# A four-layer graph network in fp32: where layer 0's bias per node is formed and added

## The chip, the cores and the metric

The kernel runs on one core of a Trainium2 chip. The metric is device time in microseconds for one launch, the median of three runs: 1666.78 us (1666.35 to 1666.91). Everything is computed in fp32.

## The reference

Eight batches of 2048 nodes with 64 features pass through four graph layers, each with a residual connection and a layer norm. `adj` is a dense 2048x2048 matrix. Only layer 0 bears on the change:

```python
def _L0_gnn_ref(x, A, embedding, weight, bias):   # K=3, D=16, 64 -> 64 features
    w = jnp.einsum('nd,dkio->nkio', embedding, weight)
    b = jnp.einsum('nd,do->no', embedding, bias)
    As = [eye(N), A, 2.0 * (A @ A) - eye(N)]
    x_g = jnp.einsum('knm,bmc->bnkc', jnp.stack(As, 0), x)
    out = jnp.einsum('bnki,nkio->bno', x_g, w)
    return out + b
...
x = _layernorm(x + _L0_gnn_ref(x, adj, ...), axis=-1)
...
x = _layernorm(x + _L1_gnn_ref(...))   # two products with adj, ReLU after each
x = _layernorm(x + _L2_gnn_ref(...))   # one product with adj, own and neighbour weights
x = _layernorm(x + _L3_gnn_ref(...))   # two products with adj
```

Each node has its own weights and its own bias, both mixed from 16 shared ones by the node's embedding. The bias of a node, `b[n]`, is a vector of 64 numbers, the same for all eight batches; it is a sum of 16 terms.

## The kernel before

**Data.** `xy` holds two copies of the node features in SBUF, slot 0 and slot 1, as 16 node tiles of 128 nodes (partitions) by 512 columns (8 batches of 64). The 8 batches are worked in 4 pairs of 128 columns. Layer 0 keeps x in slot 0, where the layer's output is gathered, and `A x` in slot 1.

**Products.** A product with `adj` uses a two-level scheme of Strassen's kind: on each level seven multiplications of sums of blocks in place of eight. The sums of adj's blocks are formed once by VectorE during the first product (`prepare`, L634) and written to DRAM (`comb`, by GpSimd's DMA queue, L649), from which all later products read them. A later product (`product`, L216) consists of seven inner products A11, S1, A12, S2, S4, S3, A22 in this order; each is seven multiplications on TensorE (L277, 3.43 us each), whose partial sums VectorE adds up from PSUM (L228) in two banks, and forms sums of x for the ones to come.

**Layer 0's first product** runs in four slices of adj (`plain_slice` for slice 0, `fast_slice` for slices 1 to 3). Its result comes out transposed and is turned back by TensorE (`to_nodes`, L465) through the pool `p_tn` of two PSUM banks, which `two_level` (L818) also uses for its partial products. Scheduling is by a planner, except where `keep_in_program_order` pins an instruction to its place on its engine.

**The bias before.** The embedding, transposed, and the 16 shared biases are loaded by ScalarE's DMA queue (L728, L733). In slice 1 TensorE forms all 16 node tiles' biases by 16 matmuls (`biases`, L737) into two banks, the pool `p_b`. In slice 3 VectorE adds them to x in four instructions of 128x2048 (`join_bias`, L766), one per quarter of x; then `centered` (L1028) takes the mean over each node's 64 features away from x, which a layer norm would do later, also on VectorE.

**Layer 0's second product and the node weights.** The second product, of slot 1, begins at the end of the slices. When an inner product has finished a quarter of the result, its four blocks are handed to `feature0` (L1090). For each of the block's four node tiles TensorE multiplies the three terms of x with the 16 shared weights, in two halves of 8, into a PSUM tile `y` (L1109; the pool `p_y` has three). VectorE scales the first half's 8 products by the node's embedding and adds them onto slot 0 (L1119). ScalarE scales the second half's 8 products into an SBUF tile `s` (L1123; two buffers), which GpSimd adds up and joins to slot 0 (L1128, L1130). The features are not mixed with the multiplications: they run in stretches after S2 (four blocks, node tiles 0 to 7, batches 0 to 3), after S3 (four, the same tiles, batches 4 to 7) and after A22 (eight blocks, tiles 8 to 15). A layer norm of two blocks follows some steps after its second block; in layer 0 GpSimd squares (L503) and VectorE does the rest.

`center` (L586) is a reduction and a subtraction on VectorE that takes the mean over the last axis away from a tile of weights; `sum_wn` (L1068) uses it for the 16 shared weights.

Of the kernel before, what the change touches and what calls it, by code (L numbers as in the profile page):

```python
# [9 lines left out]
F32 = mybir.dt.float32  # L10
AF = mybir.ActivationFunctionType
ALU = mybir.AluOpType
# [4 lines left out]
P = 128  # L17
# [87 lines left out]
def kernel(  # L105
# [4 lines left out]
    slices: bass.AP,  # L110
    blocks: bass.AP,
    emb: bass.AP,
    embT: bass.AP,
    w_l0: bass.AP,
    b_l0: bass.AP,
    w_l1: bass.AP,
# [8 lines left out]
    N = x.shape[0] * x.shape[1]  # L125
    BF = x.shape[2]
    D = emb.shape[2]
    F = b_l0.shape[1]
    B = BF // F
    NT = N // P  # L130
    NG = N // GW
# [453 lines left out]
    if True:  # L585
# [126 lines left out]
            yield  # L712

        with tc.tile_pool(name="p_n", bufs=4, space=PSUM) as p_n, tc.tile_pool(
            name="p_tn", bufs=2, space=PSUM
        ) as p_tn, tc.tile_pool(name="p_b", bufs=1, space=PSUM) as p_b, tc.tile_pool(
            name="xs", bufs=1
        ) as xs:

# [2 lines left out]
            rise = p_tn.tile([P, TG, P], F32, tag="pt", name="rise")  # L722
            for k in range(11):
                nc.tensor.matmul(rise[:, k % TG, :], zero, zero, start=True, stop=True)

            bias0 = small.tile([P, F], F32, tag="bias0", name="bias0")
            for k in range(2):
                nc.scalar.dma_start(bias0[k * F : k * F + D], b_l0)  # L728
            pb = p_b.tile([P, NT, F], F32, tag="pb", name="pb")
            e_tile = small.tile([P, TG, 4, F], F32, tag="sq", name="eT").rearrange("p t b f -> p (t b f)")  # L730
            eT = [e_tile[g // 2 * F : g // 2 * F + D, ts(g % 2, GW)] for g in range(NG)]
            for g in range(NG):
                nc.scalar.dma_start(eT[g], embT[:, ts(g, GW)])  # L733

            def biases():

                for t in (h * NT // 2 + k for k in range(NT // 2) for h in range(2)):  # L737
                    g = t // TG
                    tc.keep_in_program_order(nc.tensor.matmul(
                        pb[:, t, :], eT[g][:, ts(t % TG, P)], bias0[g // 2 * F : g // 2 * F + D],  # L740
                        start=True, stop=True,
                    ))
                yield

            def xq(h, c):

                v = xy[:, 0, h * NT // 2 : (h + 1) * NT // 2, c * 4 * F : (c + 1) * 4 * F]
                return v.rearrange("p (t h) c -> p t h c", h=2)
# [9 lines left out]
            def sums_of_x(n):  # L758
# [3 lines left out]
                    (T[2], xq(1, 1), xq(0, 1)), (T[3], xq(1, 0), T[1]),  # L762
                )[n]
                pin(nc.vector.tensor_tensor(out, a, b, ALU.subtract))

            def join_bias(h, c):  # L766
                v = xq(h, c).rearrange("p t h (b f) -> p (t h) b f", f=F)
                bias = pb[:, h * NT // 2 : (h + 1) * NT // 2, :].unsqueeze(2)
                bias = bias.to_broadcast([P, NT // 2, B // 2, F])
                tc.keep_in_program_order(nc.vector.tensor_tensor(v, v, bias, ALU.add))  # L770

            def load_chunks(ns, *js):
                if ns < TG:
# [122 lines left out]
            def fast_slice(ns, ch, held, rest):  # L896


                outers = {}
                parts = prepare(ns, ch, outers)  # L900

                def raw(I, J):
                    return lambda j, m: ch[2 * J + j][:, m, 2 * I : 2 * I + 2]

                def summed(q):
                    return lambda j, m: outers[q][:, :, j, ts(m, P)]

                def x_of(h, c):
                    return lambda k, p: xcol(0, h * NT // 2 + k, 2 * c + p)

                def t_of(n):
                    return lambda k, p: T[n - 1][:, k // 2, k % 2, ts(p, 2 * F)]

                def mul(ps, a, b, start=True, steps=2):

                    for p in range(2):
                        for k in range(NT // 2):
                            nc.tensor.matmul(  # L918
                                ps[:, ts(p, GW // 2)], b(k, p), a(k // TG, k % TG),
                                start=(start and p == k == 0), stop=(k == NT // 2 - 1),  # L920
                                skip_group_check=True,
                            )
                        if p < steps:
                            pump.step()
                    return ps

                hT = {}

                def done(blk, ps, plus):
                    ih, c = blk // 2, blk % 2  # L930
                    for p in range(2):
                        if 2 * c + p not in hT:
                            hT[2 * c + p] = new_h()
                        nc.vector.tensor_tensor(
                            hT[2 * c + p][:, ts(ih, GW // 2)], ps[:, ts(p, GW // 2)],
                            plus[:, ts(p, GW // 2)], ALU.add,
                        )

                def plus(tag, a, b):
                    u = sums.tile([P, GW], F32, tag=tag, name=tag)  # L940
                    nc.vector.tensor_tensor(u, a, b, ALU.add)
                    return u

                next(parts)
                for _ in rest:
                    pass
                next(parts)

                p2 = mul(bank(), raw(0, 1), x_of(1, 0), steps=1)
                q3 = new_out("u3")  # L950
                two_level(
                    lambda i, j: lambda m: ch[2 + j][:, m, 2 + i], outers[A22], b4, t4, by_blocks(q3)
                )
                load_chunks(ns + 1, 2, 3)
                for job in held:
                    pump.add(back(*job))
                next(parts)
                pa = mul(bank(), raw(0, 0), x_of(0, 0))
                p1 = sums.tile([P, GW], F32, tag="p1", name="p1")
                nc.scalar.copy(p1, pa)  # L960
                nc.vector.tensor_tensor(q3, q3, p1, ALU.add)
                done(0, p2, p1)
                if ns == TG - 1:
                    join_bias(0, 1)
                next(parts)
                pc = mul(bank(), summed(S1), t_of(1))
                next(parts)
                load_chunks(ns + 1, 0, 1)
                if ns == 1:
                    sum_weights(w3)  # L970
                elif ns == TG - 1:
                    join_bias(0, 0)
                pb_ = mul(bank(), summed(S2), t_of(2))
                u2 = plus("u2", pb_, p1)
                nc.vector.tensor_tensor(u2, pc, u2, ALU.add)
                nc.vector.tensor_tensor(p1, pc, p1, ALU.add)
                next(parts)
                pe = mul(bank(), summed(S4), x_of(1, 1))
                done(1, pe, u2)
                if ns == TG - 1:  # L980
                    join_bias(1, 0)
                mul(pb_, summed(S3), t_of(3), start=False)

                done(2, pb_, q3)
                done(3, pb_, p1)
                return [hT[p] for p in range(NP)]

            last_pairs = []
            for ns in range(TG):
                ch = [chunks.pop((ns, j)) for j in range(NG)]  # L990
                if ns == 0:
                    outers = {}
                    parts = prepare(ns, ch, outers)
                    for _ in range(2):
                        next(parts)
                    first4 = plain_slice(ns, ch, outers)
                    next(first4)
                    sums_of_x(0)
                    sums_of_x(1)
                    next(parts)  # L1000
                    next(first4)
                    sums_of_x(2)
                    sums_of_x(3)
                    sums_t(b4, t4)
                    next(first4)
                    next(parts)
                    hT = next(first4)
                    next(parts)
                    w3 = load_weights()
                    load_chunks(1, *AHEAD)  # L1010
                    pump.add(biases())
                else:
                    hT = fast_slice(ns, ch, held, parts if ns == 1 else ())
                for p in range(NP):
# [3 lines left out]
                for p in range(NP):  # L1018
# [3 lines left out]
                        last_pairs.append(hT[p])  # L1022
                    else:
                        pump.add(back(ns, p, hT[p]))
            join_bias(1, 1)
            pump.drain()

        def centered(h, c):  # L1028
# [13 lines left out]
        if True:  # L1042
# [11 lines left out]
                yield  # L1054

            pump.add(last_back())
            for h, c in ((0, 0), (0, 1), (1, 1), (1, 0)):
                pump.add(centered(h, c))
            e_sb = l0y.tile([P, NT, D], F32, tag="e_sb", name="e_sb")
            nc.gpsimd.dma_start(e_sb, emb)  # L1060

            wn = l0y.tile([P, 3, D, F], F32, tag="wn", name="wn")
            pieces += [
# [26 lines left out]
            def feature0(g, p, hT):  # L1090
# [7 lines left out]
                for k in range(TG):  # L1098
# [1 line left out]
                    acc = xy[:, 0, t, ts(p, 2 * F)].rearrange("p (b f) -> p b f", f=F)  # L1100


                    s = l0y.tile([P, DH, 2, F], F32, tag="s", name="s", bufs=2)
                    for h in range(2):
                        y = p_y.tile([P, 2, DH * F], F32, tag="y", name="y")
                        for n in range(3):
# [22 lines left out]
                        n //= 2  # L1129
                    nc.gpsimd.tensor_tensor(acc, acc, s[:, 0], ALU.add)  # L1130
                    yield


            RUNS = {A12: 1, S2: NP, S3: NP}
# [131 lines left out]
```

## Time and profile before

| | |
|---|---|
| median of three runs | 1666.78 us |
| the profiled execution | 1666.76 us |
| its span in the profile | 1665.0 us |
| busy in the span: PE, PEld, DVE, ACT, POOL | 1656.7, 1060.6, 965.9, 276.0, 246.1 us |
| TensorE's granted clock | 0.999 |
| slices (layer 0's first product) | 0 to 211 us |
| A11 to S2 of layer 0's second product | 211 to 309 us |
| features, four blocks | 309 to 392 us |
| S4 and S3 | 392 to 440 us |
| features, four blocks | 440 to 522 us |
| A22 and the next product's A11 | 522 to 570 us |
| features, eight blocks | 570 to 736 us |
| layers 1 to 3 | 736 to 1665 us |

The engines are PE (TensorE's matmuls), PEld (its weight loads), DVE (VectorE), ACT (ScalarE), POOL (GpSimd) and SP (a queue that here only starts DMAs). A line of the time line gives start, duration, engine, source line, operation, what it writes and reads, the shape and the count of merged instructions, and in brackets how long the engine was idle before and what it waited for. A matmul in fp32 stands in the trace as two records. In lines that group instructions, the numbers behind the bar are busy us and the mean ns of one, then the idle time before them and what ended it. In lines of a stretch stand its bounds, its length, each engine's busy time with its count, TensorE's granted clock, the DMA engines' busy share and GB/s. L12 is line 12 of the kernel.

### The profile page before, as it was taken

How to read it: one execution, taken by the hardware profiler on the slowest of the kernel's cores; microseconds unless marked ns; L12 is line 12 of the kernel's file. 1: busy time of each engine (PE TensorE's matmuls, PEld its weight loads, DVE VectorE, ACT ScalarE, POOL GpSimd, SP SyncE). 2: the span in 40 equal slices, each digit the busy share in tenths (PEclk: the TensorE clock that was granted, in tenths of full speed). 3: DMA queues.
4: the chain of work that ended last, by engine and by line, in shares of the span. 5: the costliest groups of instructions: out<-in, count | busy, mean ns of one | idle time of the engine just before them, and what ended most of it. 6: DMA issues, size and time to landing. Idle time of an engine off the chain costs nothing.

```text
span 1665.0 us, 21271 instructions
## 1 busy us (share of the span) xinstructions
PE 1656.7 (100%) x8414; PEld 1060.6 (64%) x8414; DVE 965.9 (58%) x1737; ACT 276.0 (17%) x810; POOL 246.1 (15%) x332
## 2 busy tenths in 40 slices
PE   9999999999999999999999999999999999999998
PEld 5988844444444444444454455599998455579998
DVE  5986895656456456655434365873668344453657
ACT  0200110242142144430010011220001011100001
POOL 1221200254155056550000000000000000000000
PEclk9999999999999999999999999999999999999999
DMA  8998899504503600019877867657888866678884
GB/s 318 340 383 310 316 322 326 200 26 162 205 26 129 250 26 26 26 65 364 290 266 278 304 254 257 229 218 272 291 297 299 306 209 233 230 264 294 316 311 167
DMA packets 81074, 391.56 MB, mean 235 GB/s; under 512 B 8944, under 2 KB 25584, under 8 KB 41040
## 3 DMA queue, kind: packets, MB, share of 16 engines
q1 hardware_dynamic: 68288, 346.78, 58.2%
q0 software_dynamic: 11248, 42.08, 6.7%
q10 hardware_dynamic: 1440, 1.35, 0.3%
q8 instruction: 67, 1.10, 0.3%
q14 instruction: 31, 0.25, 0.0%
HBM read 339.85 MB, written 50.33 MB: 234 GB/s over the span
## 4 chain that ended last, share of the span: by engine, by line
PE 95%; DVE 3%; DMA 1%; issue 0%; SPq 0%; DVEq 0%
PE y L1109 20%; PE mmb L277 17%; PE mma L277 12%; PE mmc L277 12%; PE mmb L270 9%; PE ps_n L918 7%; PE mma L270 6%; PE mmc L270 6%; PE z L1161 3%; PE z L1190 2%; PE ps_i L832 1%; DVE si L640 1%; DMA xy<-in_x 1%; PE pt L1152 1%; DMA bias<-in_b_l 0%; DVE so L640 0%
## 5 line engine op out<-in xcount | busy, mean ns | idle before, releaser
L277 PE MATMUL mmb<-a,t 128*128 128x512 f32 x648 | 292.0, 593 | 0.0
L1119 DVE SCALAR_TENSOR_TENSOR xy<-y,e_sb,xy 128x128 f32<-128x128 f32 x512 | 179.6, 351 | 141.2 <-PE y L1109 125.3
L277 PEld LDWEIGHTS mmb<-a,t 128*128 128x128 f32 x648 | 121.5, 190 | 145.3 <-issue 143.5
L1128 POOL TENSOR_TENSOR s<-s 128x512 f32<-128x512 f32 (+2 forms) x192 | 157.4, 820 | 333.0 <-ACT s L1123 322.8
L1123 ACT ACTIVATE s<-y,e_sb 128x128 f32<-128x128 f32 x512 | 139.3, 383 | 231.5 <-PE y L1109 231.5
L228 DVE TENSOR_TENSOR u<-mmb,p 128x512 f32<-128x512 f32 x84 | 57.9, 689 | 176.5 <-PE mmb L277 121.1
L270 PE MATMUL mmb<-t,a 128*128 128x128 f32 x1344 | 156.9, 275 | 0.0
L270 PEld LDWEIGHTS mmb<-t,a 128*128 128x128 f32 x1344 | 153.5, 192 | 0.0
L1109 PE MATMUL y<-wn,xT 64*128 64x512 f32 x512 | 131.5, 590 | 0.0
L1109 PE MATMUL y<-wn,C 64*128 64x512 f32 x512 | 131.2, 589 | 0.0
L1109 PE MATMUL y<-wn,tT 64*128 64x512 f32 x512 | 131.2, 589 | 0.0
L277 PE MATMUL mma<-a,T 128*128 128x512 f32 x256 | 115.5, 594 | 0.0
L277 PE MATMUL mmc<-a,t 128*128 128x512 f32 x216 | 97.3, 592 | 0.0
L295 ACT COPY p<-mma 128x512 f32<-128x512 f32 x42 | 24.7, 588 | 405.8 <-PE mma L277 248.4
L1109 PEld LDWEIGHTS y<-wn,xT 64*128 64x128 f32 x512 | 49.3, 187 | 61.2 <-issue 60.7
L1109 PEld LDWEIGHTS y<-wn,tT 64*128 64x128 f32 x512 | 49.6, 187 | 60.2 <-issue 60.2
L1109 PEld LDWEIGHTS y<-wn,C 64*128 64x128 f32 x512 | 49.5, 187 | 60.3 <-issue 60.3
L277 PE MATMUL mma<-a,xy 128*128 128x512 f32 x192 | 86.6, 594 | 0.3 <-PE pt_n L465 0.3
L277 PEld LDWEIGHTS mma<-a,T 128*128 128x128 f32 x256 | 47.6, 190 | 56.8 <-issue 56.5
L228 DVE TENSOR_TENSOR C<-mmc,C 128x512 f32<-128x512 f32 x48 | 33.2, 692 | 85.9 <-PE mmc L277 75.1
L277 PEld LDWEIGHTS mmc<-a,t 128*128 128x128 f32 x216 | 40.0, 190 | 45.4 <-issue 45.2
L277 PEld LDWEIGHTS mma<-a,xy 128*128 128x128 f32 x192 | 36.0, 190 | 44.4 <-issue 43.8
(160 smaller groups left out, 2127.5 us busy)
## 6 DMA issues: line engine op xcount, KB each, us to landing
a<-comb SPq DMA_DIRECT2D x240, 1024.0 KB, 4.8
a<-in_blocks SPq DMA_DIRECT2D x54, 1024.0 KB, 4.8
comb<-si POOLq DMA_DIRECT2D x28, 1024.0 KB, 6.2
a<-in_slices SPq DMA_DIRECT2D x15, 1024.0 KB, 9.0
comb<-so POOLq DMA_DIRECT2D x15, 512.0 KB, 9.6
t1T<-hT SPq DMA_DIRECT2D x16, 256.0 KB, 4.6
xT<-in_xT SPq DMA_DIRECT2D x16, 256.0 KB, 3.0
tT<-t1T SPq DMA_DIRECT2D x16, 256.0 KB, 3.1
```

The lines of the kernel that those rows point to most:

```text
L228: nc.vector.tensor_tensor(out, a, b, op)
L270: nc.tensor.matmul(to, a[:, k, m, :], xb[:, m, :], start=(start and opens and m == 0), stop=(m == TG - 1), skip_group_check=True,)
L277: nc.tensor.matmul(ps, xb[:, m, :], a[:, :, m, :], start=(start and m == 0), stop=(m == TG - 1), skip_group_check=True,)
L295: nc.scalar.copy(p1, pa)
L640: tc.keep_in_program_order(nc.vector.tensor_tensor(out, a, b, op))
L918: nc.tensor.matmul(ps[:, ts(p, GW // 2)], b(k, p), a(k // TG, k % TG), start=(start and p == k == 0), stop=(k == NT // 2 - 1), skip_group_ ...
L1109: mm = nc.tensor.matmul(y[:, b, :], terms[n][half, ts(k, P)], wn[half, n, h * DH : (h + 1) * DH, :], start=(n == 0), stop=(n == 2),)
L1119: nc.vector.scalar_tensor_tensor(acc, y[:, :, ts(d, F)], e, acc, ALU.mult, ALU.add)
L1123: nc.scalar.activation(s[:, d], y[:, :, ts(d, F)], AF.Copy, scale=e)
L1128: nc.gpsimd.tensor_tensor(s[:, :n], s[:, :n], s[:, n : 2 * n], ALU.add)
L1161: nc.tensor.matmul(z[:, k, :], aT[:, ts(k, P)], wd[:, w, :], start=(n == 0), stop=(n == len(terms) - 1),)
L1190: nc.tensor.matmul(z[n][:, k], xT[half, ts(k, P)], w[half], start=True, stop=True)
```

## The change

TensorE's bias matmuls, VectorE's joins and the loads of the transposed embedding go. A generator `biased(h)` takes their place, once per half of the node tiles. It takes two of the buffers `s`, loads the 16 shared biases, each repeated on all partitions, into the first (512 KB, GpSimd's DMA queue), has VectorE centre them, and then for each of 8 node tiles lets GpSimd multiply them with the node's embedding into the second, add the 16 terms up in four halving steps, and add the result to all eight batches of that tile in slot 0. The first half is queued among the `centered` steps during A11; the second after the fourth block's features, that is between the first stretch of features and S4. x is centred before the bias is added and the bias by itself. The two banks of `p_b` go to `p_tn`, which has four. The function `new_s` is the allocation that stood in `feature0`.

```diff
@@ -712,8 +711,8 @@
         with tc.tile_pool(name="p_n", bufs=4, space=PSUM) as p_n, tc.tile_pool(
-            name="p_tn", bufs=2, space=PSUM
-        ) as p_tn, tc.tile_pool(name="p_b", bufs=1, space=PSUM) as p_b, tc.tile_pool(
+            name="p_tn", bufs=4, space=PSUM
+        ) as p_tn, tc.tile_pool(
             name="xs", bufs=1
         ) as xs:
@@ -722,26 +721,6 @@
-            bias0 = small.tile([P, F], F32, tag="bias0", name="bias0")
-            for k in range(2):
-                nc.scalar.dma_start(bias0[k * F : k * F + D], b_l0)
-            pb = p_b.tile([P, NT, F], F32, tag="pb", name="pb")
-            e_tile = small.tile([P, TG, 4, F], F32, tag="sq", name="eT").rearrange("p t b f -> p (t b f)")
-            eT = [e_tile[g // 2 * F : g // 2 * F + D, ts(g % 2, GW)] for g in range(NG)]
-            for g in range(NG):
-                nc.scalar.dma_start(eT[g], embT[:, ts(g, GW)])
-
-            def biases():
-
-                for t in (h * NT // 2 + k for k in range(NT // 2) for h in range(2)):
-                    g = t // TG
-                    tc.keep_in_program_order(nc.tensor.matmul(
-                        pb[:, t, :], eT[g][:, ts(t % TG, P)], bias0[g // 2 * F : g // 2 * F + D],
-                        start=True, stop=True,
-                    ))
-                yield
@@ -762,12 +741,6 @@
-            def join_bias(h, c):
-                v = xq(h, c).rearrange("p t h (b f) -> p (t h) b f", f=F)
-                bias = pb[:, h * NT // 2 : (h + 1) * NT // 2, :].unsqueeze(2)
-                bias = bias.to_broadcast([P, NT // 2, B // 2, F])
-                tc.keep_in_program_order(nc.vector.tensor_tensor(v, v, bias, ALU.add))
@@ -960,16 +933,12 @@
-                if ns == TG - 1:
-                    join_bias(0, 1)
...
@@ -1008,7 +975,6 @@
-                    pump.add(biases())
@@ -1022,7 +988,6 @@
-            join_bias(1, 1)
             pump.drain()
@@ -1054,10 +1019,33 @@
             pump.add(last_back())
-            for h, c in ((0, 0), (0, 1), (1, 1), (1, 0)):
-                pump.add(centered(h, c))
             e_sb = l0y.tile([P, NT, D], F32, tag="e_sb", name="e_sb")
             nc.gpsimd.dma_start(e_sb, emb)
+
+            def new_s():
+                return l0y.tile([P, DH, 2, F], F32, tag="s", name="s", bufs=2)
+
+            def biased(h):
+
+                b, terms = (new_s().rearrange("p a b f -> p (a b) f") for _ in range(2))
+                nc.gpsimd.dma_start(b.rearrange("p d f -> p (d f)"), b_l0.to_broadcast([P, D * F]))
+                center(b, pin=tc.keep_in_program_order)
+                for t in range(h * NT // 2, (h + 1) * NT // 2):
+                    e = e_sb[:, t].unsqueeze(2).to_broadcast([P, D, F])
+                    nc.gpsimd.tensor_tensor(terms, b, e, ALU.mult)
+                    n = D // 2
+                    while n:
+                        nc.gpsimd.tensor_tensor(terms[:, :n], terms[:, :n], terms[:, n : 2 * n], ALU.add)
+                        n //= 2
+                    acc = xy[:, 0, t].rearrange("p (b f) -> p b f", f=F)
+                    nc.gpsimd.tensor_tensor(acc, acc, terms[:, :1].to_broadcast([P, B, F]), ALU.add)
+                yield
+
+            for h, c in ((0, 0), (0, 1)):
+                pump.add(centered(h, c))
+            pump.add(biased(0))
+            for h, c in ((1, 1), (1, 0)):
+                pump.add(centered(h, c))
@@ -1100,7 +1088,7 @@
-                    s = l0y.tile([P, DH, 2, F], F32, tag="s", name="s", bufs=2)
+                    s = new_s()
@@ -1129,6 +1117,10 @@
                     nc.gpsimd.tensor_tensor(acc, acc, s[:, 0], ALU.add)
                     yield
+                if (g, p) == order[TG - 1]:
+
+                    for _ in biased(1):
+                        pass
```

## The prediction

> **What bounds the kernel now.** I read the chain of waits first, then TensorE's waits, then busy time by stretch, and last the time line where GpSimd and VectorE meet. The chain:
>
> ```profile
> PE 95%; DVE 3%; DMA 1%; issue 0%; SPq 0%; DVEq 0%
> ```
>
> TensorE sets the end. Its waits in all 1665.0 us (us in total, times, longest):
>
> ```profile
> PE rise L724 <- DVE zero L721: 1.1, 1, 1.1
> PE ps_i L832 <- DVE si L640: 0.3, 1, 0.3
> PE mma L277 <- PE pt_n L465: 0.3, 1, 0.3
> ```
>
> So whatever leaves another engine buys nothing unless TensorE gets shorter, and whatever makes TensorE wait is paid in full. The new work lands in these stretches (products A11 to S2, features, products S4 and S3, features; busy us of PE, PEld, DVE, ACT, POOL):
>
> ```profile
> 211.00:309.00 98.00, 97.73 (x237) 43.62 (x237) 70.05 (x75) 5.61 (x9) 0.00 (x0) 1.00 0.91 324
> 309.00:392.00 83.00, 83.00 (x385) 37.28 (x386) 46.20 (x130) 33.97 (x121) 45.45 (x61) 1.00 0.14 44
> 392.00:440.00 48.00, 48.00 (x114) 21.15 (x114) 27.13 (x44) 3.56 (x12) 5.45 (x5) 1.00 0.79 286
> 440.00:522.00 82.00, 82.00 (x384) 36.85 (x382) 45.27 (x128) 32.66 (x120) 44.76 (x60) 1.00 0.11 36
> ```
>
> POOL is empty in the first and nearly empty in the third, which invites work; but VectorE is busy for 70 and 27 us there. Whether the two run side by side is shown where they meet today, at 396 us (VectorE's time line, then GpSimd's):
>
> ```profile
> 396.54 1.38 DVE L228 TENSOR_TENSOR C<-C,p 128x512 f32<-128x512 f32 x1 [0.69 <-ACT p L295]
> 398.66 0.69 DVE L228 TENSOR_TENSOR u<-mmb,p 128x512 f32<-128x512 f32 x1 [0.74 <-PE mmb L277]
> 399.27 0.84 DVE L228 TENSOR_TENSOR t<-T,t 128x512 f32<-128x512 f32 x1
> 400.04 2.37 DVE L228 TENSOR_TENSOR C<-C,u 128x512 f32<-128x512 f32 x1
> ```
> ```profile
> 396.11 2.93 POOL L1128 TENSOR_TENSOR s<-s 128x512 f32<-128x512 f32 x3 [4.16 <-ACT s L1123]
> 399.12 0.45 POOL L1130 TENSOR_TENSOR xy<-xy,s 128x128 f32<-128x128 f32 x1
> 399.65 2.22 POOL L503 TENSOR_TENSOR sq<-xy 128x1024 f32<-128x1024 f32 x1
> ```
>
> A 128x512 add of two SBUF tiles takes 0.68 to 0.69 us elsewhere (C<-C,u at 407.46: 0.68). Here it takes 2.37, and ends 0.54 after the GpSimd square (399.65 + 2.22 = 401.87) does. The square takes 2.22 instead of the 1.89 of those that meet nobody: it waited for t<-T,t. The add u<-mmb,p, with one input in PSUM, stays at 0.69 under a GpSimd instruction. So a VectorE instruction with two SBUF inputs and a GpSimd instruction take turns, each waiting for the whole of the other.
>
> **What leaves TensorE.** Slice 1 loses the 16 bias matmuls:
>
> ```profile
> 62.51 2.00 PE L739 MATMUL pb<-bias,eT 16*128 16x64 f32 x32
> 64.44 3.72 PE L918 MATMUL ps_n<-a,xy 128*128 128x256 f32 x16
> 68.00 1.05 PE L832 MATMUL ps_i<-a,xy 128*128 128x128 f32 x8
> 69.37 1.13 PE L832 MATMUL ps_i<-si,t 128*128 128x128 f32 x8 [0.31 <-DVE si L640]
> ```
>
> They hold it for 64.44 - 62.51 = 1.93 us. But at 69.37 TensorE waits for VectorE's si, and VectorE is busy 32.65 of the 33 us from 35 to 68, so si comes no earlier. What counts is the work that the changed order puts ahead of that wait: four transposes (0.43), one ps_n matmul (3.55 / 8 = 0.44) and three of ps_i (0.89 x 3 / 4 = 0.67), together **1.5 us**. More, up to 1.9, if six loads less (four eT, two bias, 136 KB, 0.4 us at the first stretch's 339 GB/s) let VectorE start earlier; 0 if later loads, with the DMA engines all busy from 68 to 130, give it back. I take 1.5. The four banks do no more: no transpose waits for a bank in the waits above. The four joins on VectorE (L770, 2.28 us each, 9.1) were on nobody's path; the one at 211.53 only lengthens an idle time before 217.38.
>
> **What GpSimd gets.** `biased` runs twice, for 8 node tiles each: a product 128x1024, adds of 512, 256, 128 and 64, a join of 128x512. Rows:
>
> ```profile
> L1128 POOL TENSOR_TENSOR s<-s 128x512 f32<-128x512 f32 x64 | 81.1, 1268 | 322.9 <-ACT s L1123 322.8
> L1128 POOL TENSOR_TENSOR s<-s 128x256 f32<-128x256 f32 x64 | 47.1, 736 | 5.0
> L1128 POOL TENSOR_TENSOR s<-s 128x128 f32<-128x128 f32 x64 | 29.2, 456 | 5.0
> L503 POOL TENSOR_TENSOR sq<-xy 128x1024 f32<-128x1024 f32 x8 | 15.8, 1976 | 0.6
> ```
>
> No row has a 1024-wide product of two different tiles. Below: the square of one tile, 1.89. Above: two 512-wide adds, 2.54. The adds grow by 2.12 ns per element (0.725 undisturbed at 256, 1.268 at 512), which continues to 2.35 at 1024 and 0.32 at 64; I take these, since the product reads two tiles as the adds do. A node tile is 2.35 + 1.27 + 0.73 + 0.46 + 0.32 + 1.27 + 6 gaps of 0.08 = 6.87 us, eight are **55 us**.
>
> The Trainium skill ("GPSIMD Engine Reference", 3.1 Elementwise) gives 4497 ns for a two-input add of 2048 fp32, laying it to the read port; an estimate from it for 1024 is 2.33, against 1.89 in the only row of that width here. By the page the sum below is 23 us before the gain, by that row 17.
>
> VectorE also centres the bias tile twice (a reduction 1.21 and a subtraction 1.22, as wn's at L589 and L590). The reduction waits for the bias load, and behind it on VectorE stand the reads that free TensorE's banks. SP's queue keeps its order.
>
> I laid VectorE, GpSimd and TensorE on one time line in the changed order, with taking turns; TensorE advances by 3.43 us per multiplication and waits for VectorE's read of its bank, which has 3.43 - 0.2 - 0.69 - 0.05 = 2.5 us to spare. Without `biased` this gives features at 308.7 and 439.6 (trace: 308.89, 439.75).
>
> *First half, 211 to 309.* GpSimd starts at 233.7, after the centring. VectorE has no idle time there until 248.8. Centring makes it 2.3 late, its next eight two-input operations wait 0.99, 0.06, 0.39, 0.25, 0.84, 1.20, 0.66 and 0.39 (4.8), and some 1.9 of idle absorbs part: S1's u is 5.2 late, 2.5 are spare, TensorE stalls 2.7. At wn's sums (from 285) the waits are 0.16, 0.66, 1.01, 2.28, 0.07: S2's first u stalls it 2.3; then 1.21 and 2.28 stall it 3.5. Together **8.5 us**. The join ends near 312, features start at 317, so they don't wait for it.
>
> *Second half, from 392.* GpSimd first has its adds and the square, so `biased` starts at 402.9. Centring and waits of 1.85 and 2.28 make VectorE free S4's bank late: 3.6 us. Then GpSimd needs 55.0 plus 16 turns of 0.53 lent to VectorE, until 466.4. It holds both s buffers, the first until its last product, 462.0. Features start at 439.6 + 3.6 = 443.1, 2.58 us per y. With three y buffers the fifth y (due at 453.4) needs that of the second, which ScalarE can't read before it has an s: 462.0 + 0.2 + 2.2 = 464.4. That is 10.9 us more, **14.5 us** in this half. The bias load is queued on POOL before the last tile's adds and should land near 396.3 (4.6 us, as t1T's 256 KB); at the 9.6 of a 512 KB comb write the half costs 1.2 more. The first load goes ahead of two comb writes whose queue idles 3.70 and 1.77 us before them, so it hides.
>
> Sum 23.0. Such turns fall by chance: with GpSimd 5% faster the line gives 18.0, 5% slower 23.0, gaps of 0.05 give 21.6, and if scalar_tensor_tensor (in no row beside GpSimd) takes no turns, 19.3. The mean of the five is 21.0. **21.0 - 1.5 = 19.5 us.** The profiled execution took 1666.76 (span 1665.0), the median 1666.78: **1686.3 us**. Its own range: 17.0 - 1.9 (product at 1.89) to 26.0 + 1.2 (2.54, late load, no gain), 1682 to 1694.
>
> **Rivals.**
> - *No turns in these rows' sense* (the product or the small adds leave VectorE alone). Then only the s buffer is late: `biased` ends near 456, costs 4.4, net +2.9: 1669.7. Against it stand the 2.37 and 1.38. Chance 0.06.
> - *Not slower: GpSimd's work hides.* Place: the s buffers at 462. From 402.9 to 451 plus the last tile's 4.4 after its product there are 52.5 us; less the 8.5 lent, a tile of 5.5 us or less decides it, with VectorE's waits inside the 2.5 us. Time 1665.3. For it: an empty POOL. Against: 6.87, and 6.4 even with the square's 1.89. Chance 0.05.
> - *The broadcast operand costs more.* At 3.5 for the product, half as much again, the line gives 36.3: 1701.6. No row shows a broadcast on GpSimd. Chance 0.08.
>
> **How the numbers follow.** The forecast has 0.81. 0.2% is 3.3 us, about what a measurement of this kernel tells from no change. The first two rivals lie within it, 0.11, of which I give 0.01 to faster (the second with a larger gain) and leave 0.10 to no change; the forecast and the third rival are slower, 0.89. The range takes the forecast's own and the chance of the turns on both sides: 1676 to 1696.
>
> **What would show it.** No L739, ps_i waiting longer for si; `C<-C` and `t` adds of VectorE between 236 and 300 at a mean above 1 us against 0.69; TensorE waiting for VectorE in S1 and S2, some 8 us; GpSimd's join ending near 466 and TensorE's y waiting for ScalarE, ScalarE for GpSimd, some 11 us after 450. It is wrong if VectorE's adds stay at 0.69, or if a node tile takes less than 5.5 us.

## The result, and the profile after

| | before | after |
|---|---|---|
| median | 1666.62 us (1666.35 to 1666.91, 4 runs) | 1678.67 us (1677.85 to 1678.87, 4 runs) |
| profiled execution, span | 1666.76, 1665.0 | 1677.85, 1676.1 |
| granted TensorE clock | 0.999 | 0.997 |

The ratio is 1.0071, with a 95% interval of [1.0054, 1.0089]: slower by 12.1 us in the medians, by 11.1 in the spans. The forecast was 19.5 us. The same views as before, now of the kernel after: the chain of waits, then TensorE's waits (total, times, longest), then its stretches (length, and busy us of PE, PEld, DVE, ACT, POOL, then clock, DMA share, GB/s), cut where they now begin and end.

```profile
PE 79%; POOL 3%; DVE 1%; issue 0%; ACT 0%; POOLq 0%; DVEq 0%
```
```profile
PE y L1097 <- ACT s L1111: 4.0, 1, 4.0
PE mmc L276 <- DVE C L227: 2.8, 2, 2.0
PE mmb L276 <- DVE u L227: 1.9, 2, 1.2
```
```profile
209.00:310.00 101.00, 97.96 (x232) 43.06 (x232) 83.36 (x74) 5.30 (x9) 67.38 (x48) 1.00 0.90 314
310.00:392.60 82.60, 82.60 (x385) 37.10 (x384) 45.73 (x129) 33.85 (x121) 44.91 (x60) 1.00 0.12 38
392.60:444.90 52.30, 50.32 (x116) 21.77 (x114) 40.65 (x46) 3.55 (x12) 45.93 (x39) 0.97 0.77 273
444.90:533.50 88.60, 84.58 (x386) 37.65 (x385) 46.23 (x130) 32.57 (x120) 60.39 (x77) 0.98 0.11 35
```

GpSimd has entered the chain that ends last, and TensorE has five new waits. VectorE is busy for 83.36 us of the first stretch and 40.65 of the third, against 70.05 and 27.13 before, although one centring of 2.4 us each is all that came to it there (and a join left the first): the rest is time in which its instructions wait. In the last two rows the clock column is below 1, which none of the same stretches of before shows.

Where the time went, by the starts of TensorE's phases in the two time lines:

| | before | after | difference | forecast (before variants) |
|---|---|---|---|---|
| slices, until the first multiplication of A11 | 211.71 | 209.26 | -2.45 | -1.5 |
| A11 to S2 | 97.18 | 100.76 | +3.58 | +8.5 |
| features 1 | 82.60 | 82.60 | 0 | 0 |
| S4 and S3 | 48.26 | 52.21 | +3.95 | +3.6 |
| features 2 | 82.61 | 88.59 | +5.98 | +10.9 |

All the rest together gives less than 0.1. Slice 1 shows what left TensorE (its time line after):

```profile
62.23 0.60 PE L464 MATMUL pt_n<-ident,hT 128*128 128x128 f32 x4
...
67.01 0.60 PE L891 MATMUL ps_n<-a,xy 128*128 128x256 f32 x2
67.58 0.94 PE L805 MATMUL ps_i<-a,xy 128*128 128x128 f32 x6
68.43 1.16 PE L805 MATMUL ps_i<-si,t 128*128 128x128 f32 x8
```

The L739 rows are gone, four transposes, a ps_n and some ps_i multiplications stand ahead of the ones that read si, as the prediction listed. But the first ps_i that reads si starts at 68.43 without a wait, where it waited 0.31 until 69.37: VectorE is earlier, too.

The turns in the first half (VectorE, GpSimd and TensorE after, around S1's u):

```profile
246.34 1.75 DVE L227 TENSOR_TENSOR t<-xy 128x512 f32<-128x512 f32 x1
248.01 2.81 DVE L436 TENSOR_TENSOR T<-xy 128x2048 f32<-128x2048 f32 x1
251.60 0.68 DVE L227 TENSOR_TENSOR u<-mmb,p 128x512 f32<-128x512 f32 x1
...
244.34 7.51 POOL L1038 TENSOR_TENSOR s<-s 128x512 f32<-128x512 f32 x4
...
252.34 3.70 PE L276 MATMUL mmb<-a,t 128*128 128x512 f32 x8 [0.76 <-DVE u L227]
```

The 128x512 add takes 1.75 instead of 0.68, the 128x2048 one 2.81 instead of 2.28, and GpSimd's four halving adds, 2.99 when alone, 7.51. The u add with its PSUM input is as fast as ever; it comes too late, and TensorE waits 0.76 for it.

The s buffer in the second half (GpSimd, ScalarE and TensorE after):

```profile
455.26 1.90 POOL L1035 TENSOR_TENSOR s<-s,e_sb 128x1024 f32<-128x1024 f32 x1
...
457.19 2.17 ACT L1111 ACTIVATE s<-y,e_sb 128x128 f32<-128x128 f32 x8 [32.22 <-POOL s L1035]
...
459.42 1.36 PE L1097 MATMUL y<-wn,xT 64*128 64x512 f32 x4 [4.02 <-ACT s L1111]
460.56 1.92 PE L1097 MATMUL y<-wn,tT 64*128 64x512 f32 x4
```

The last product of `biased` ends at 457.16 and frees the first s; ScalarE starts at 457.19 and is through at 459.36; the fifth y starts at 459.42, 4.02 late. What follows is slow as well: four matmuls take 1.92 us instead of 1.02. The clock has been halved.

### The profile page after: what moved, and what is told of

Same layout as the page of the kernel before. It is cut to its first block, busy times and chain, and to the rows that moved or that the text cites. A ratio compares the mean times of both kernels' runs of the same rounds, so it can differ in the third digit from the quotient of the medians.

```text
span 1676.1 us, 21320 instructions
## 1 busy us (share of the span) xinstructions
PE 1659.3 (99%) x8382; PEld 1059.3 (63%) x8382; DVE 986.1 (59%) x1737; ACT 275.4 (16%) x810; POOL 368.9 (22%) x430
## 4 chain that ended last, share of the span: by engine, by line
PE 79%; POOL 3%; DVE 1%; issue 0%; ACT 0%; POOLq 0%; DVEq 0%
PE y L1097 19%; PE mmb L276 15%; PE mmc L276 10%; PE mma L276 9%; PE mmb L269 9%; PE mma L269 6%; PE mmc L269 6%; PE z L1153 3%; PE z L1182 2%; POOL s L1038 1%; POOL s L1035 1%; PE pt L1144 1%; POOL xy L1041 1%; DVE wn L589 0%; ACT s L1111 0%
```

## The experiments

Starts and lengths in this table are read from the time lines as above; the times are medians. The kernel before, run beside them, had 1666.56, 1666.58 and 1666.57 us. Each time line is that of one execution; those of e4 and e8 took 1679.40 and 1669.42 us, 1.0 and 1.8 above their medians.

| kernel | A11 starts | A11 to S2 | S4, S3 | features 2 | median, us |
|---|---|---|---|---|---|
| e1 no bias | 209.09 | 97.17 | 48.27 | 82.60 | 1664.86 |
| e3 GpSimd only writes | 209.05 | 97.18 | 49.17 | 88.98 | 1671.87 |
| e4 two banks | 209.65 | 100.74 | 50.65 | 91.33 | 1678.43 |
| e5 loads kept | 210.11 | 100.74 | 52.35 | 89.47 | 1679.25 |
| e6 bias among the features | 210.73 | 97.17 | 48.26 | 84.87 | 1672.51 |
| e7 longer tile | 208.98 | 101.12 | 49.22 | 94.88 | 1681.52 |
| e8 before, loads on GpSimd's queue | 214.30 | 97.18 | 48.27 | 82.60 | 1667.65 |
| e9 as e6, tiles unbroken | 210.49 | 97.18 | 48.27 | 82.60 | 1666.42 |

### e1: is it all GpSimd's new work?

```diff
-            pump.add(biased(0))
...
-                    for _ in biased(1):
-                        pass
```

> Both calls of biased are left out, so the output lacks layer 0's bias. If all of the loss after 209 us comes from that GpSimd work (theory): the products A11 to S2 fall back from 100.8 to 97.2 us, S4 and S3 from 52.2 to 48.3, the second features from 88.6 to 82.6, the clock stays at 1.0 throughout, and the earlier start stays: span 1676.1 - 13.5 = 1662.6, time 1664.3. Rival (part of the loss comes from the changed order itself, for example the centring steps now split around biased): some of the stretches keep 1 us or more, time above 1666.

Measured 1664.86 us, span 1662.7, ratio to before 0.9989 [0.998, 0.9999]. Every stretch is back at its length of before and the clock is whole. All that is lost after 209 us comes from `biased`: its load, its centring on VectorE and its work on GpSimd, which e1 takes away together and e3 tells apart; what the change takes from the slices is worth the 1.7 us by which this kernel beats the one before.

### e3: turns, or anything GpSimd does?

```diff
-                    nc.gpsimd.tensor_tensor(terms, b, e, ALU.mult)
...
+                    for k in range(7):
+                        nc.gpsimd.memset(b if last and k == 0 else terms, 0.0)
```

> Product, adds and join of each node tile are replaced by seven memsets of the same scratch tiles (128x1024, an estimated 0.97 us each from the 0.85 of the 896-wide memset of wd), so GpSimd is occupied for about 58 us in each half as after, both s buffers are held as after, the load and the centring stay, but GpSimd reads no SBUF; the output lacks the bias. Theory (VectorE's instructions with two SBUF inputs take turns only with a GpSimd instruction that reads): VectorE's 128x512 adds stay at 0.69, A11 to S2 fall back to 97.2 us and S4 and S3 to 48.3, while the s buffer is released at about 456 and costs some 6.6 us plus 1.7 of halved clock in the second features: time 1671 to 1674. Rival 1 (any GpSimd work holds VectorE up, or the queue, load and centring do it): first half and S4 keep 3.6 and 3.9: about 1679. Rival 2 (the s buffer is not what the features wait for): the second features fall back to 82.6, about 1665.

Measured 1671.87 us, ratio 1.0034 [1.0021, 1.0047], the theory's time. Its VectorE around S4, then GpSimd and VectorE just before:

```profile
L227 DVE TENSOR_TENSOR t<-T,t 128x512 f32<-128x512 f32 x4 | 3.8, 961 | 0.0
L227 DVE TENSOR_TENSOR C<-C,u 128x512 f32<-128x512 f32 x4 | 2.7, 683 | 0.0
```
```profile
397.87 1.89 POOL L502 TENSOR_TENSOR sq<-xy 128x1024 f32<-128x1024 f32 x1
399.70 55.21 POOL L1036 MEMSET s<- 128x1024 f32 x55
...
398.50 1.80 DVE L227 TENSOR_TENSOR t<-T,t 128x512 f32<-128x512 f32 x1
400.23 0.68 DVE L227 TENSOR_TENSOR C<-C,u 128x512 f32<-128x512 f32 x1
...
402.07 0.51 DVE L515 TENSOR_SCALAR ss<-ss 128x16 f32<-128x16 f32 x1
```

The same two groups of after, from 403.4 to 444.8:

```profile
L227 DVE TENSOR_TENSOR C<-C,u 128x512 f32<-128x512 f32 x4 | 7.7, 1931 | 0.0
L227 DVE TENSOR_TENSOR t<-T,t 128x512 f32<-128x512 f32 x4 | 5.6, 1390 | 0.0
```

Under 55 us of memsets the adds C<-C,u take 683 ns; under 55 us of products and sums they take 1931. In e3 the only slow one of the group t<-T,t, 1.80, lies beside the square, which reads, at 397.87. So reading is what takes turns. The load and the centring are still there in e3, and A11 to S2 are at their length of before. The stall of S4 shrinks from 3.95 to 0.9 us, behind the centring and the add beside the square, and the wait of the features for an s stays (3.44 us, then two windows of halved clock). In the first half the memsets didn't wait for the centring and were through at 256, so there e3 covers S1 and not S2.

The Trainium skill ("SBUF — State Buffer", Who interferes with whom) says the same: a VectorE instruction with two SBUF inputs contends with a GpSimd instruction that reads SBUF, not with one that only writes; 683 against 1931 agrees. It also says that tensor_scalar may enter a two-port mode in which it contends with GpSimd; the 128x16 one above took 0.51 beside a memset, and 0.17 in after (at 407.54), where it started in the gap between two GpSimd adds. The 128x1024 one, which has a single SBUF input, takes 0.69 in before (286.82) and 2.28 in after, beside a product of GpSimd, the longest of the waits ahead of S2's first u:

```profile
285.40 2.28 DVE L1059 TENSOR_SCALAR wn<-wn 128x1024 f32<-128x1024 f32 x1
```

### e4 and e5: what started A11 earlier?

e4 gives `p_tn` two banks. e5 brings the six loads back, with nobody reading them.

```diff
-            name="p_tn", bufs=4, space=PSUM
+            name="p_tn", bufs=2, space=PSUM
```
```diff
+            for k in range(2):
+                nc.scalar.dma_start(bias0[k * F : k * F + D], b_l0.rearrange("o (d f) -> (o d) f", f=F))
...
+            for g in range(NG):
+                nc.scalar.dma_start(eT[g], embT[:, ts(g, GW)])
```

> The pool of transposes has two banks again, all else as after. Theory (the earlier start comes from the matmuls and loads that left, not from the banks): the first product starts at 209.3 as after, within 0.4; time 1678.7. Rival (four banks bring part of it): it starts at 210.3 or later, 1679.7 or more.

> The six loads of embT and the bias go out from ScalarE's queue again, as before the change, and nobody reads them; all else as after. Theory (1.0 of the 2.45 us of the slice phase comes from the loads that no longer stand in front of SP's second slice load, 1.5 from the matmuls): SP's second slice load is issued at about 8.0 again instead of 5.1, VectorE's first si add starts at about 15.5 instead of 14.3, and the first product starts at about 210.2 instead of 209.3. Rival (the matmuls alone): it stays at 209.3.

e4 has A11 at 209.65, 0.39 later than after, and in its slices a wait of 0.4 us for a load of x that after doesn't show; its time is 1678.43. The banks bring nothing that can be told from such a load. e5 has A11 at 210.11, 0.85 later; its time line (SP's second slice load, and TensorE at the first si):

```profile
8.14 0.33 SPq L158 DMA_DIRECT2D a<-in_slices  x1
...
69.28 1.16 PE L814 MATMUL ps_i<-si,t 128*128 128x128 f32 x8 [1.33 <-DVE si L640]
```

In after that load is issued at 5.11 and there is no wait. So the 2.45 us split into 1.60 for the matmuls (211.71 - 210.11; the three joins that stood in slice 3 go with them, and no run parts the two) and 0.85 for the loads, behind which SP's second slice load is issued 3 us later. None of these three time lines shows a wait for x; A11's start scatters by 0.3 us among after, e1, e3 and e7, whose slices are the same.

### e8: the loads of the kernel before on another queue

```diff
-                nc.scalar.dma_start(eT[g], embT[:, ts(g, GW)])
+                nc.gpsimd.dma_start(eT[g], embT[:, ts(g, GW)])
```

(and the two bias loads likewise.)

> The kernel before, with its six loads of embT and bias issued from GpSimd's queue instead of ScalarE's; all else as before. Theory (these loads stand ahead of SP's slice loads): SP's second slice load is issued at about 5 instead of 8.0, VectorE's first si add starts at 14.3 instead of 15.5, TensorE's wait of 0.31 at 69.37 goes and the first product starts at about 211.2 instead of 211.7: time 1666.1, 0.5 less. Rival (the loads' bytes, not their queue): nothing moves.

A miss: 1667.65 us, ratio 1.0004 [0.9996, 1.0013]. SP's second slice load does go out at 5.17, but VectorE's first si add starts at 15.95, no earlier than before's 15.50, and TensorE waits for x:

```profile
11.49 25.77 PE L872 MATMUL ps_n<-a,xy 128*128 128x512 f32 x56 [2.43 <-DMA xy<-in_x]
```

The queue explains when the slice load is issued, not when the first data are all there. So the 0.85 us of the loads stand, by e5, but that they are the price of the order of issue is not shown. Waits for x of 0 to 1.7 us also show in kernels whose slices are the same instructions as after's, e4 but for its banks (after, e1, e3, e7: none; e4 0.4; e9 0.8; e10 1.2; e6 1.7). What sets them stays open; differences of the slices below about 1.5 us between two kernels are to be read only with that wait beside them.

### e7 and e10: the price of the tile

e7 adds one 128x128 add on scratch to each node tile, which was meant to bring it to 6.95 us.

```diff
+                    nc.gpsimd.tensor_tensor(terms[:, 8:10], terms[:, 8:10], terms[:, 10:12], ALU.add)
```

> One more GpSimd add (128x128, 0.46 and a gap of 0.08) per node tile on scratch, which makes a tile 6.95 us, the 6.87 of the prediction in place of the measured 6.42; all else as after. If the only thing the prediction mis-sized is the tile (theory): the first half loses 8.5 us where after loses 3.6, the y waits for s grow from 4.0 by some 4.5 us and halve the clock once more: time 1686. Rival (the prediction's time line overstates the turns too): the first half stays below 6 us, the y wait grows by about 4 (8 tiles of 0.54) and the clock by 1.7: 1683 to 1685.

Measured 1681.52 us, ratio 1.0086 [1.0072, 1.01]: less than either expected. A11 to S2 lose 3.9 us, hardly more than in after, S4 loses only 1.0, and the wait for s has grown to 9.71:

```profile
462.20 2.08 PE L1098 MATMUL y<-wn,xT 64*128 64x512 f32 x4 [9.71 <-ACT s L1112]
```

But the tile has not become as long as both expectations had it. Undisturbed it takes 6.68 us (451.35 to 458.03) against 6.39 in after (448.87 to 455.26), 0.29 more and not 0.54, since the added add (L1040) overlaps its neighbours by 0.04 where the others leave a gap of 0.08:

```profile
451.35 1.90 POOL L1035 TENSOR_TENSOR s<-s,e_sb 128x1024 f32<-128x1024 f32 x1
453.33 2.06 POOL L1038 TENSOR_TENSOR s<-s 128x512 f32<-128x512 f32 x2
455.35 0.45 POOL L1040 TENSOR_TENSOR s<-s 128x128 f32<-128x128 f32 x1
455.76 0.85 POOL L1038 TENSOR_TENSOR s<-s 128x128 f32<-128x128 f32 x2
...
458.03 1.90 POOL L1035 TENSOR_TENSOR s<-s,e_sb 128x1024 f32<-128x1024 f32 x1
```

So e7 puts back 0.29 of the 0.48 us by which the prediction's 6.87 was too long, and neither expectation is put to the test. Features 2 lose 12.3 us, but much of that has only moved there from S4, since GpSimd decides when the buffer comes free. S4's loss, the wait for s and 0.27 (see the account of the stalls below) together make 10.94 us, against 8.24 in after: 2.7 more, where eight tiles of 0.29 are 2.3. The first half has 0.4 more. So the tile's length reaches the s buffer in full and the first half hardly.

e10 prices the row itself: to e9 below it adds 18 GpSimd instructions behind the last features.

```diff
+                    for op in (ALU.add, ALU.mult):
+                        for other in (w, e, u):
+                            for _ in range(3):
+                                tc.keep_in_program_order(nc.gpsimd.tensor_tensor(w, u, other, op))
```

> Added work only, to price the prediction's mis-sized row: as e9_unbroken, and after the last features, when GpSimd has nothing more to do, 18 more of its 128x1024 instructions on the two s buffers, three of each: a sum of two tiles, of a tile and the embedding repeated 64 times, of a tile with itself, and the same three as products. The undisturbed minimum of each three counts. Theory A (a second full tile costs, a repeated operand or the same tile twice does not): sum and product of two tiles 2.35 to 2.54, the other four 1.9. Theory B (the operation costs: products 1.9, sums more): all sums 2.35 or more, all products 1.9. Theory C (the width alone: above 512 an element costs less): all six 1.9. TensorE doesn't wait for these; the time stays within 2 us of e9_unbroken's 1666.4, or more if the next layer's tiles wait for the two buffers.

Of its GpSimd time line, the first sums (of two tiles, three instructions) and the last products (of a tile with itself); then the product with the repeated embedding among the features of e9 (310 to 390 us; busy us, mean ns):

```profile
745.69 7.23 POOL L1143 TENSOR_TENSOR s<-s 128x1024 f32<-128x1024 f32 x3
...
783.35 6.16 POOL L1143 TENSOR_TENSOR s<-s 128x1024 f32<-128x1024 f32 x3
```
```profile
L1037 POOL TENSOR_TENSOR s<-bc,e_sb 128x1024 f32<-128x1024 f32 x4 | 7.6, 1905 | 0.0
```

The three sums of two tiles took 2.35, 2.35 and 2.37 us, the products of two tiles 2.34 and 2.35 (and one 4.27), those of a tile with itself 1.89 at best, sums and products alike. The ones with the embedding took 2.23 at best here, where VectorE was at work beside them; undisturbed among the features the product takes 1.905. That is theory A: a second full tile costs 0.45 us at this width, a repeated operand doesn't (its sum has no undisturbed row). The time of this kernel, run once, is 1694.02 and says nothing of the prices; that TensorE wouldn't wait was wrong, it waited 14.9 us for blocks of adj and 6.6 for VectorE.

### e6 and e9: the same work where it doesn't meet

GpSimd's instructions stay; their places change, and the shared biases, now in the square's tile, are loaded and centred three times instead of twice. Tiles 4 to 7 run after all four centring steps, the others one by one among the features, after their 2nd, 5th, 8th and 11th node tile. e9 differs from e6 in one point.

```diff
+                    if block < 3 and entry * TG + k in (1, 4, 7, 10):
+                        bias_tile(biases[block], (0, 3, 2)[block] * TG + (entry * TG + k) // 3)
```
```diff
-                nc.gpsimd.tensor_tensor(terms, b, e, ALU.mult)
+                pin(nc.gpsimd.tensor_tensor(terms, b, e, ALU.mult))
```

(`pin` is `keep_in_program_order`, set on the adds and the join, too.)

> The same GpSimd instructions, placed elsewhere: tiles 4 to 7 before the first features, after all four centring steps; one tile after the 2nd, 5th, 8th and 11th of the 16 node tiles of the features 1, 2 and 3, where VectorE reads PSUM in most of its instructions and TensorE needs 5.16 us per node tile against GpSimd's 2.8, so that three tiles leave 7 us for a 6.4 us bias tile. b lies in the square's tile, each terms tile takes its turn in the two s buffers. Theory (the loss is the turns with VectorE's two-input adds plus the s buffers): S4 and S3 48.3, features 2 82.7, no halved clock, the first products at most 1 us above 92.8: time 1664.9 to 1666.0, below the kernel before. Rival (any GpSimd work beside the features holds s buffers up): features 1 to 3 grow by 1 us or more each, time above 1668.

e6: 1672.51 us, the rival's time. The products lose nothing in either half, but features 1, 2 and 3 grow by 1.9, 2.3 and 2.3 us. GpSimd and ScalarE in features 1:

```profile
318.96 1.90 POOL L1036 TENSOR_TENSOR s<-bc,e_sb 128x1024 f32<-128x1024 f32 x1
320.94 3.00 POOL L1039 TENSOR_TENSOR s<-s 128x512 f32<-128x512 f32 x4
323.90 1.26 POOL L1126 TENSOR_TENSOR s<-s 128x512 f32<-128x512 f32 x1
325.13 1.26 POOL L1042 TENSOR_TENSOR xy<-xy,s 128x512 f32<-128x512 f32 x1
...
326.42 2.18 ACT L1121 ACTIVATE s<-y,e_sb 128x128 f32<-128x128 f32 x8 [5.67 <-POOL xy L1042]
```

The planner put an add of the next feature tile (L1126) ahead of the bias tile's join (L1042), so the buffer came free 1.26 us later, and TensorE had a wait of about 0.3 at nearly every bias tile (11 waits, 3.3 us; with 0.27 for each, see below, 6.3 of the 6.5). e9 tests that:

> As e6_in_features, with the six GpSimd instructions of a bias tile held together, so that no add of the next feature tile slips in between them. There the terms tile was released 7.45 us after its product began (318.96 to 326.4), ScalarE stood 5.67 us before its next s, and TensorE lost about 0.5 us per bias tile in the features. Theory (the order on GpSimd alone causes that): the release comes 6.4 us after the product begins, ScalarE is 1.0 us less late, inside what three y buffers allow (2 x 2.58 - 2.2 = 3.0 us), features 1, 2 and 3 take 82.7 us each, no y waits for ScalarE: 1664.9 to 1666.0, 0.5 to 1.7 less than the kernel before. Rival (two s buffers are too few for any bias tile among the features): features 1 to 3 still grow by 1 us or more each, time above 1668.

e9: 1666.42 us, ratio to before 0.9997 [0.9988, 1.0006]; its features:

```profile
309.00:392.00 83.00, 83.00 (x384) 37.28 (x381) 46.16 (x130) 33.95 (x121) 68.53 (x85) 1.00 0.13 41
441.00:524.00 83.00, 83.00 (x381) 37.26 (x378) 49.04 (x135) 33.27 (x123) 68.91 (x85) 1.00 0.12 35
```

TensorE is busy throughout, beside 68 us of GpSimd's work in each. All the bias now hides: from A11's start to the end of the span it takes 1453.3 us (1663.8 - 210.49), as the kernel before (1665.0 - 211.71). It is 12 us faster than after and can't be told from before; the bound is e1's 1664.86, and what is missing to it lies in the slices (A11 starts 1.4 us later), 0.8 of it the open wait for x. The theory's 1664.9 to 1666.0 is missed by 0.4.

## Why the prediction was right, and where it was too large

- **The sign and the places** held: TensorE waits for VectorE in S1, S2 and S4 and for ScalarE in the second features, and e1 shows that nothing else is lost.
- **The matmuls' 1.5 us**: 1.60 by e5. The "up to 1.9" for the loads was too low: I priced them by their bytes (0.4), and they cost 0.85 (e5), how is open (e8). "si comes no earlier" failed through them: with the loads gone ps_i does not wait for si at all; with them back (e5) it waits 1.33, longer than before, as I had said.
- **Four banks and joins**: nothing that can be told, as said (e4; for the joins, e1, where A11 to S2 take 97.17 without the one at 211.53; the three before it are in e5's 1.60).
- **The turns** are real, and for adds of two SBUF tiles they are with GpSimd's reads, not its writes (e3). scalar_tensor_tensor takes them as well, as my main line had it against one variant: 2.54 us at 236.30 in after against 2.28 in before. "With two SBUF inputs" was too narrow: the tensor_scalar at 285.40, with one, waited 1.59.
- **The product at 2.35** is the step that failed in the s buffer's term. The extrapolation from adds was exact for two tiles (e10: 2.35), but this product reads one tile and a repeated operand and costs 1.90, as the square, which I had named as the lower bound. Eight tiles are 3.6 us shorter. The buffer came free at 457.16; features 1 start 1.13 us later than before, which the forecast's 462.0 doesn't have, so on its scale that is 456.0, 6.0 earlier. The other 2.4 are an earlier start of `biased` (0.55) and, mostly, fewer turns: from 403.48 to 457.16 GpSimd takes 7 us more than undisturbed tiles would (an estimate with 6.39 each), where I had 8.5. The chain behind it was right: 2.4 us from release to y forecast, 2.26 measured.
- **The first half at 8.5** failed in another step: the single waits on the hand-drawn time line. Up to S1's u they sum to 3.0 us in after (0.50, 0.26, 0.12, 0.26, 1.07, 0.53, 0.26), where I had 4.8; before S2's u 2.9 (1.59, 0.54, 0.75) for 4.2; before its bank 1.07 for 3.5. With the centring's 2.3, less 1.9 of idle and the 2.5 to spare, that leaves 0.9 (measured: a wait of 0.76) where I had 2.7. The tile doesn't account for it: with 0.29 of the 0.48 put back, e7 loses 3.9. The likely reading, which no run tests, is that each wait is what happens to be left of GpSimd's instruction when VectorE's comes up, and that my line and its variants were all unlucky by comparison. That a line laid by hand should err on this side is not explained.
- **S4 at 3.6**: 3.95, but by luck. The wait is 1.98, and 1.70 are the halved clock, which the prediction didn't have. e4 and e5, with the same instructions there, show 2.4 and 4.1, e7 1.0. It matters little, as the release of the buffer fixes the sum: S4's loss, the wait for s and its 0.27 make 8.24 us in after, 8.47 in e4 and 8.38 in e5, where I had 14.5.
- **Left out**: the halved clock, 1.7 us twice, and 0.27 us that each stall costs beyond the wait that the trace shows. 0.17 of these are how the wait is counted: an undisturbed multiplication has a line of 3.60 though the next starts after 3.43, and the wait begins at the line's end. 0.10 are lost behind the stall: at 252.34 the next one starts after 3.53 instead of 3.43. So 0.76 + 1.19 + 0.83 + 3 x 0.27 = 3.59 is the first half's 3.58, 1.98 + 1.70 + 0.27 = 3.95 is S4's, and 4.02 + 1.70 + 0.27 = 5.99 the features'.
- **The rivals**: "no turns" falls by e3. "It hides" named a tile of 5.5 us as the condition; e9 shows that the place decides, with the tile at 6.4. "The broadcast operand costs more" had the wrong sign.

The measured time lies in the low part of the range and below the forecast's own 1682 to 1694: both mis-sized terms erred upwards. That it isn't lower still owes something to luck, since the halved clock, which the prediction didn't have, adds to the loss: an estimate is 1.7 us net, the features' window, as without S4's the wait for s would be longer by as much.

## What to carry to other kernels

An empty GpSimd is not free room: ask whether VectorE reads two SBUF tiles there, and put GpSimd's reading work where VectorE reads PSUM, as e9 does, or let it only write. When such work borrows buffers, follow their release to the engine that needs them next, and keep the group that holds one unbroken on its engine. Price a GpSimd instruction by a row with the same operands, not only the same width.

## What the runs showed of the hardware

TensorE's clock is halved for whole windows of 3.41 us, one, two or three among the products and features of after, e3, e4, e5 and e7 (3.41, 6.83 and 10.24 us), and what decides is TensorE's idle time in the window just before. Three windows of after, each with the one that follows, then the one of e4 that stayed whole and its follower (length, PE busy first, clock in the column after POOL):

```profile
405.59:409.00 3.41, 1.43 (x4) 0.49 (x3) 3.31 (x7) 0.22 (x1) 3.10 (x5) 1.00 0.84 300
409.00:412.41 3.41, 3.41 (x5) 1.35 (x4) 3.34 (x6) 0.00 (x0) 3.25 (x3) 0.50 0.53 221
453.37:456.79 3.42, 2.03 (x10) 0.58 (x6) 2.35 (x7) 0.00 (x0) 3.18 (x4) 1.00 0.00 0
456.79:460.20 3.41, 0.78 (x4) 0.49 (x6) 0.00 (x0) 2.17 (x8) 3.10 (x5) 1.00 0.00 0
460.20:463.61 3.41, 3.41 (x10) 1.39 (x8) 0.00 (x0) 2.00 (x8) 3.24 (x4) 0.50 0.00 0
```
```profile
407.40:410.81 3.41, 1.70 (x4) 0.87 (x5) 3.24 (x8) 0.21 (x1) 3.10 (x5) 1.00 0.83 317
410.81:414.22 3.41, 3.41 (x9) 1.52 (x8) 3.41 (x4) 0.00 (x0) 3.33 (x2) 1.00 0.30 65
```

A window with 1.98 us idle (3.41 - 1.43) or 2.63 is followed by a halved one, one with 1.39 or, in e4, 1.71 is not; e4's wait was longer (2.12 us) but fell across two windows. Once the clock is halved, less keeps it so: in e3 a halved window with 1.41 idle (455.75 to 459.16) is followed by a second one. So a wait of 2 us costs 1.7 more or nothing here, by where it falls. The Trainium skill ("TensorE: Matmul & The Clock Gate", What's actually happening) has the free-running window of 3413 ns, which these runs show; it has the clock drop after at least one idle window, and here 1.98 us idle of 3.41 were enough, so the measurement decides against a whole one.

The second unexpected thing is how stalls replace each other. After, e4 and e5 run the same code from A11 on; e4 lost 1.6 us less in S4, for want of a halved window there, and 2.7 more in features 2, because the buffer's release is set by GpSimd: TensorE came earlier, waited longer (5.81 us) and lost two windows of clock instead of one.
